# A fused layernorm, banded attention and fp8 linear kernel: another order of loads, other ranks, groups and engine roles

## The chip, the core and the metric

The kernel runs on one core of one Trainium2 chip. The core has five engines with an instruction queue each: TensorE (PE), VectorE (DVE), ScalarE (ACT), GpSimd (POOL) and SyncE (SP), and 16 DMA engines that they share. Each engine takes its instructions in the order in which they were written; between engines semaphores keep the order. The metric is the device time of the kernel in microseconds (us), as the median of several runs. A profiled execution gives the trace from which the tables are read.

## The reference, cut to what matters

```
xn   = layernorm(x)                                   # x: 8 x 512 rows of 1024 float32
attn = einsum('ds,td->st', w1, w2) * sparse_mask      # 1024 x 1024, a band around the diagonal
a    = gelu(einsum('bds,st->bdt', xn, attn) + b2)     # exact gelu
w_q  = fp8_e4m3(weight * 448 / max|weight|)           # one scale for the whole weight
x_q  = fp8_e5m2(xn * 57344 / max|xn|)                 # one scale for all of xn
f    = einsum('bsk,nk->bsn', x_q, w_q) * (1/x_scale) * (1/w_scale) + bias
out  = x + a + f
```

Two maxima are global: the linear part of any row can start only when the largest absolute value of all 4096 normalized rows is known, and the weight can be rounded only when the largest weight is known.

## The kernel before

The 4096 rows are 32 tiles of 128 rows and 1024 columns. Tiles 0 to 15 are *early*: they are loaded once, normalized, transposed, and multiplied by the attn band while the loading goes on. Tiles 16 to 31 are *late*: they are loaded for their statistics and their maximum only, given back, and loaded again when their turn comes.

The work has three stages. In the first, SP loads the x tiles and eight chunks of w1, w2 and the mask; PE makes the band of attn from them, eight chunks of float32 matmuls (`attn_matmuls`, L296), and DVE multiplies each chunk by its mask (`attn_mask`, L307). In the second, the products of the early tiles (`product_matmul`, L518) fill PE, while the maxima of the tiles (`row_max`, L399) and of the weight (`weight_amax`, L448) are taken and the weight is rounded to fp8 values held in bf16. In the third, PE goes through all 32 tiles with the fp8 linear (`linear_matmul`, L558, accumulator `pf`), in 32 steps; the products and transposes of the late tiles are woven into these.

Nothing of this order is written out directly. The kernel lists its operations with an engine, a cost, a rank, what they come after, and which buffers they take and free (`do` of the class `Plan`). `Plan.order` walks through a modelled time and gives each free engine the ready operation of lowest rank; the operations are then emitted in this order, and each engine's queue on the chip is fixed by it. A cost, a lag or a rank changes no computation, only the place in the queues.

The names that the change and the steps below touch:

- `load_order` (L74) gives the order of the loads: for each of the eight attn chunks the chunk, two early x and one late x, with two early x ahead of everything; then the weight once for its maximum ("once"), then again for its rounding ("twice") between late x. Each attn chunk is three loads: w1, the new columns of w2, and the mask.
- `GROUPS` (L35) says which tiles get their inverse root together. The first and last group take it on DVE with one power on POOL (`variance` L336, `power` L340, `inverse_root` L346 to L348, `shifts` L351); the others run eight small instructions on POOL (`inverse_root_gpsimd`, L360 to L369).
- `BY_SCALAR`: early tiles that ACT normalizes (`normalize`, L385); POOL normalizes the others (`normalize_gpsimd`, L394).
- `BY_VECTOR`: early tiles whose second transposed half is moved out of PSUM by DVE (`evict_by_vector`, L505) and not by ACT (`evict_transposed`, L502).
- `B2_BY_TENSOR`: early tiles whose accumulator is started by a matmul with b2 (`b2_matmul`, L513) and not by a copy of ACT (`preload`, L509).
- `ROUNDED_BY_VECTOR`: weight chunks that DVE rounds (L467, L468) and not POOL (`weight_rounded`, L472, L473). Both come after ACT's scaling (L454) and DVE's `weight_magic` (L460, L463).
- `STREAM`: how many late x and "once" weights the planner lets be held at a time.
- `late_amax` (L440), `amax_rows` (L410, which writes `x_mine`), `amax_transpose` (L415, `pt_x`), `amax_row`, `amax_back` and `scale_and_inverse` are the steps to the scale of x. They hop between DVE and PE; `quantize` (L551) and `descale` (L444) follow.

PE's queue holds the transpose `pt_x` in the middle of the early products, and `shifts` of the last group stands on DVE ahead of the steps to the maximum:

```
if lo == 0 or hi == TILES:
    op = do(V, 0.2, 0 if lo == 0 else 99, shifts, lo, hi, after=(op,))
```

Of the kernel before, what the change touches and what calls it, by code (L numbers as in the profile page):

```python
# [23 lines left out]
EARLY = 16  # L24
SLOTS = 34
QUANT = 4
STREAM = 5
LATE = 4

SQUARED = range(EARLY, EARLY + 8)  # L30
BY_VECTOR = range(EARLY // 2, EARLY-5)
B2_BY_TENSOR = range(11, EARLY)
ROUNDED_BY_VECTOR = (6,7)
BY_SCALAR = range(0, 2)
GROUPS = [(0, 2), (2, 4), (4, 8), (8, 12), (12, EARLY), (EARLY, EARLY + 8), (EARLY + 8, 28), (28, 32)]  # L35
TINY = 1e-36
# [35 lines left out]


def load_order():  # L74

    late = iter([*SQUARED, *(i for i in range(EARLY, TILES) if i not in SQUARED)])
    early = iter(range(EARLY))
    found = [("x", next(early)), ("x", next(early))]
    for sc in range(NC):
        found += [("attn", sc)]  # L80
        found += [("x", i) for i in (next(early, None), next(early, None)) if i is not None]
        found += [("x", next(late))]
    found += [("once", c) for c in range(NC)]
    for c in range(NC):
        found += [("twice", c), ("x", next(late))]
    return found
# [90 lines left out]
def banded_path(  # L177
# [264 lines left out]
    def descale():  # L442
        v["descale"] = const.tile([P, 1], F32, name="descale")
        nc.vector.tensor_mul(v["descale"], v["x"][1], v["w"][1])  # L444

# [214 lines left out]
    def more(kind, k):  # L660
        if kind == "x":
            x_ops[k] = load(1.4, load_x, k, take=("slot",) if k < EARLY else ("slot", "stream"))
        elif kind == "attn":
            attn_ops[k] = load(3.0 if k else 3.8, load_attn, k, take=("slot",))
        elif kind == "once":
            w_once[k] = load(1.4, load_weight, k, take=("slot", "stream"))
        else:
            w_twice[k] = load(1.4, load_weight, k, take=("slot", "twice"), after=(w_once[NC - 1],), lag=4.0)

# [19 lines left out]
    for i in range(TILES):  # L689
        if i in SQUARED:  # L690
            m = do(A, 1.6, 5 + 0.01 * i, mean_of, i, after=(x_ops[i],))
            stat[i] = do(A, 1.4, 4, squares, i, after=(m,))
        else:
            stat[i] = do(V, 1.43, 4 + 0.01 * i, statistics, i, after=(x_ops[i],))
    for lo, hi in GROUPS:
        group = [stat[i] for i in range(lo, hi)]
        if 0 < lo and hi < TILES:
            op = do(G, 1.7 + 0.16 * (hi - lo), 0, inverse_root_gpsimd, lo, hi, after=group)
        else:
            op = do(V, 0.2, 0, variance, lo, hi, after=group)  # L700
            op = do(G, 0.4 + 0.16 * (hi - lo), 0, power, lo, hi, after=(op,))
            op = do(V, 0.6, 0, inverse_root, lo, hi, after=(op,))
        for i in range(lo, hi):
            root[i] = shifted[i] = op
        if lo == 0 or hi == TILES:
            op = do(V, 0.2, 0 if lo == 0 else 99, shifts, lo, hi, after=(op,))
            for i in range(lo, hi):
                shifted[i] = op
    maxima, normal, settled = {}, {}, {}
    for i in range(EARLY):  # L710
        if i in BY_SCALAR:
            normal[i] = do(A, 1.14, 3 + 0.01 * i, normalize, i, after=(shifted[i],))
        else:
            normal[i] = do(G, 1.2, 3 + 0.01 * i, normalize_gpsimd, i, after=(shifted[i],))
        maxima[i] = do(V, 1.15, 3 + 0.01 * i, row_max, i, after=(normal[i],))

        settled[i] = do("later", 0.0, i, lambda: None, lag=2.0, after=(normal[i],))
    for i in range(EARLY, TILES):
        ready = stat[i]
        if i not in SQUARED:  # L720
            ready = do(A, 1.14, 3.5, mean_minus, i, after=(ready,))
        maxima[i] = do(V, 1.15, 3 + 0.01 * i, row_max_late, i, after=(ready,), free=("slot", "stream"))
    squared = do(
# [8 lines left out]
    def global_amax(name, fp8_max, rank, cols, after, lag=0.1):  # L732
# [8 lines left out]
    sums = [  # L741
        do(V, 1.15, 2, weight_amax, c, after=(w_once[c],), free=("slot", "stream")) for c in range(NC)
    ]
# [3 lines left out]
    for c in range(NC):  # L747
        op = do(A, 1.1, 1, weight_scaled, c, after=(w_known, w_twice[c]))
# [17 lines left out]
    for i in range(EARLY):  # L766
        in_big = i >= EARLY - NC
        for q in range(2):
# [457 lines left out]
```

## Time and profile before

| what | value |
|---|---|
| median of 3 runs | 317.58 us (317.0 to 317.83) |
| the profiled execution's own time | 316.91 us |
| its span, first to last instruction | 315.0 us |
| mean granted TensorE clock | 0.997 |
| busy: PE, DVE, ACT, POOL | 288.9, 232.0, 158.4, 134.2 us |
| first matmul of attn | 9.98 us |
| first linear matmul (`pf`) | 128.11 us |
| read from and written to HBM | 56.60 and 16.78 MB |

Busy time is the sum of an engine's instructions in the span; PE's matmuls are pipelined, so their lengths overlap a little and a start-to-start distance is the better price of one. A wait is written as the engine and line that stood idle, an arrow, and what ended the idle time, with the total, the number of times and the longest. In the timeline each line gives start and length in us, the engine, the line of the kernel, the operation, and output and input tiles with their shapes. In the rows by window each engine's busy time is followed by the number of its instructions.

### The profile page before, as it was taken

To read this page: it belongs to the slowest core of one execution; us is meant where nothing else is said; L and a number is where in the kernel's file an instruction comes from. 1 tells how busy PE (TensorE), PEld (TensorE's weight loads), DVE (VectorE), ACT (ScalarE), POOL (GpSimd) and SP (SyncE) were. 2 spreads that over 40 slices of the span, in tenths; PEclk is the share of its full clock that TensorE was granted. 3 is DMA by queue.
4 is the path that set the end of the run, shared out by engine and by line. 5 is a ranking of instruction groups with operands and counts; after the bars stand their busy time and mean duration, and the time that the engine had idled before them with its cause. 6 is when DMAs were issued, how large, how long until landed. Compare 5 with 4: busy or idle time off the path is not lost.

```text
span 315.0 us, 4363 instructions
## 1 busy us (share of the span) xinstructions
PE 288.9 (92%) x1563; PEld 216.6 (69%) x1563; DVE 232.0 (74%) x343; ACT 158.4 (50%) x255; POOL 134.2 (43%) x165
## 2 busy tenths in 40 slices
PE   2668889998999979999999999999999999999992
PEld 0657667897998858776676676676667667667651
DVE  3587698999999989756577667767767755766582
ACT  1368369585999956743344424533534442452200
POOL 3151707988488789666311311320331131131160
PEclk9999999999999999999999999999999999999998
DMA  7999999999636747999999987653153332221313
GB/s 251 404 385 379 388 391 390 395 422 417 247 102 230 232 169 108 211 210 271 306 278 305 358 356 236 234 200 135 67 200 135 115 125 99 114 86 67 135 68 141
DMA packets 28509, 73.74 MB, mean 234 GB/s; under 512 B 3392, under 2 KB 11840, under 8 KB 28480
## 3 DMA queue, kind: packets, MB, share of 16 engines
q1 hardware_dynamic: 20992, 47.17, 40.7%
q0 software_dynamic: 2592, 9.44, 15.0%
q10 hardware_dynamic: 4896, 16.78, 13.2%
q8 instruction: 14, 0.23, 0.3%
q14 instruction: 15, 0.12, 0.1%
HBM read 56.60 MB, written 16.78 MB: 233 GB/s over the span
## 4 chain that ended last, share of the span: by engine, by line
PE 59%; DVE 18%; DMA 10%; SPq 5%; ACT 2%; issue 2%; POOL 2%; POOLq 0%
PE pf L558 34%; PE py L518 19%; DMA w<-in_w_dram 8%; DVE row_amax L399 5%; PE pt L493 4%; SPq L262 4%; DVE st L313 3%; DVE w_cols L448 2%; DMA x<-in_x_dram 2%; SPq L253 1%; DVE magic L463 1%; DVE magic L460 1%; PE pa L296 1%; POOL w L472 1%; ACT x L528 1%
## 5 line engine op out<-in xcount | busy, mean ns | idle before, releaser
L558 PE MATMUL pf<-wq,xqts 128*128 128x512 bf16 x504 | 147.8, 379 | 0.0
L518 PE MATMUL py<-attn,xnt 128*128 128x268 f32 (+2 forms) x480 | 117.4, 340 | 2.9 <-ACT py L509 1.6
L518 PEld LDWEIGHTS py<-attn,xnt 128*128 128x128 f32 x480 | 86.7, 190 | 25.7 <-ACT py L509 1.8
L543 POOL TENSOR_TENSOR x<-x,gelu 128x512 f32<-128x512 f32 x32 | 40.8, 1274 | 125.3 <-ACT gelu L540 123.8
L585 DVE SCALAR_TENSOR_TENSOR pf<-pf,descale,bias_bc 128x512 f32<-128x512 f32 x62 | 46.9, 756 | 53.1 <-PE pf L558 53.1
L558 PEld LDWEIGHTS <-xqts 128*128 128x128 fp8e5 x504 | 49.8, 101 | 22.7 <-issue 0.2
L540 ACT ACTIVATE gelu<-py 128x512 f32<-128x512 f32 x32 | 19.1, 598 | 76.5 <-PE py L518 76.5
L588 DVE TENSOR_TENSOR x<-pf,x 128x512 f32<-128x512 f32 x62 | 42.9, 692 | 4.4 <-DVE pf L585 0.5
L399 DVE TENSOR_REDUCE row_amax<-x 128x1 f32<-128x1024 f32 x32 | 37.5, 1200 | 4.5 <-POOL x L394 3.1
L296 PE MATMUL pa<-w_sb,w 128*128 128x268 f32 (+1 forms) x128 | 30.2, 391 | 9.5 <-DMA w_sb<-in_w2t_dram 9.5
L313 DVE BATCH_NORM_STATS2 st<-x 128x6 f32<-128x512 f32 x48 | 30.3, 673 | 9.3 <-DMA x<-in_x_dram 9.3
L502 ACT COPY xnt<-pt 128x512 f32<-128x512 f32 x48 | 27.2, 581 | 16.7 <-PE pt L493 16.7
L296 PEld LDWEIGHTS pa<-w_sb,w 128*128 128x128 f32 x128 | 24.5, 200 | 14.8 <-issue 11.5
L493 PE MATMUL pt<-ident,xn 128*128 128x128 f32 x128 | 33.7, 273 | 0.0
L518 PE MATMUL py<-attn,xnt_big 128*128 128x198 f32 (+2 forms) x160 | 33.2, 343 | 0.0
L509 ACT COPY py<-b_bc 128x512 f32<-128x512 f32 x54 | 32.0, 601 | 1.0
L518 PEld LDWEIGHTS py<-attn,xnt_big 128*128 128x128 f32 x160 | 26.7, 190 | 2.9 <-issue 0.3
L493 PEld LDWEIGHTS pt<-ident,xn 128*128 128x128 f32 x128 | 17.9, 141 | 13.8
L385 ACT ACTIVATE xn<-x,shift,rstd 128x1024 f32<-128x1024 f32 x16 | 19.8, 1240 | 12.9 <-DVE x L588 8.2
L528 ACT ACTIVATE x<-py 128x512 f32<-128x512 f32 x32 | 18.6, 600 | 6.9 <-PE py L518 6.8
L551 DVE TENSOR_SCALAR xqts<-xnt,x_scale 128x1024 fp8e5<-128x1024 f32 x24 | 21.5, 896 | 0.0
L493 PE MATMUL pt<-ident,x 128*128 128x128 f32 x128 | 18.7, 274 | 2.6 <-ACT xnt L502 1.9
(103 smaller groups left out, 239.0 us busy)
## 6 DMA issues: line engine op xcount, KB each, us to landing
x<-in_x_dram SPq DMA_DIRECT2D x48, 512.0 KB, 7.6
out_dram<-x ACTq DMA_DIRECT2D x31, 512.0 KB, 2.6
w<-in_wt_dram SPq DMA_DIRECT2D x16, 512.0 KB, 8.5
x<-in_x_dram POOLq DMA_DIRECT2D x16, 512.0 KB, 19.3
w<-in_w_dram SPq DMA_DIRECT2D x8, 512.0 KB, 9.0
mask<-in_mask_dram SPq DMA_DIRECT2D x8, 512.0 KB, 8.0
w_sb<-in_w2t_dram SPq DMA_DIRECT2D x6, 512.0 KB, 10.7
attn<-in_mask_dram SPq DMA_DIRECT2D x6, 134.0 KB, 9.2
```

The costliest lines, as they stand in the source:

```text
L296: nc.tensor.matmul(pt[:, : hi - lo], w1_sb[:, c, :], w2_sb[:, c, lo:hi], start=(c == 0), stop=(c == NC - 1),)
L313: nc.vector.bn_stats(st[:, h, :], xs[i][:, half(h)])
L399: nc.vector.tensor_reduce(row_amax[:, i : i + 1], xs[i], AX.X, ALU.max, apply_absolute_value=True)
L493: nc.tensor.transpose(pts[i, q][:, j, :], xn[:, c * P : (c + 1) * P], ident)
L502: nc.scalar.copy(xnts[i][:, q * (NC // 2) : (q + 1) * (NC // 2), :], pts.pop((i, q)))
L509: nc.scalar.copy(pys[i, h], b2_bc[:, half(h)])
L518: nc.tensor.matmul(pys[i, h][:, lo - h * HALF : hi - h * HALF], xnts[i][:, sc, :], attn[:, sc, lo - band(sc)[0] : hi - band(sc)[0]], start ...
L528: nc.scalar.activation(xs[i][:, half(h)], pys.pop((i, h)), AF.Gelu)
L543: nc.gpsimd.tensor_add(xs[i][:, half(h)], xs[i][:, half(h)], gelus[i][:, half(h)])
L558: nc.tensor.matmul(v["pf", i, h], v["quant"][:, xqts[i], c, :], wq[:, c, half(h)], start=(c == 0), stop=(c == NC - 1),)
L585: nc.vector.scalar_tensor_tensor(pf, pf, v["descale"], v["bias"][:, half(h)], ALU.mult, ALU.add)
L588: nc.vector.tensor_add(res[:, half(h)], pf, res[:, half(h)])
```

## The change

The loads follow a string of 56 letters: four early x and a late one come ahead of attn's first chunk, and further on early x, late x, attn chunks and weight loads are mixed in another way. The first group of two tiles is split in two groups of one. ACT normalizes seven early tiles in place of two. DVE moves out the second half of nine early tiles in place of three. Four tiles (8, 9, 11, 12) start from a b2 matmul in place of five. DVE rounds weight chunks 5 and 7 in place of 6 and 7. `descale` is written as a multiplication by a scalar column and comes behind the first quantization, and the shift of the last group comes behind the scale of x, with a rank between the quantizations. Ranks, lags and the size of `STREAM` differ.

```diff
-STREAM = 5
+STREAM = 6
-BY_VECTOR = range(EARLY // 2, EARLY-5)
-B2_BY_TENSOR = range(11, EARLY)
-ROUNDED_BY_VECTOR = (6,7)
-BY_SCALAR = range(0, 2)
-GROUPS = [(0, 2), (2, 4), (4, 8), (8, 12), (12, EARLY), (EARLY, EARLY + 8), (EARLY + 8, 28), (28, 32)]
+BY_VECTOR = (2, 6, 7, 8, 10, 11, 12, 14, 15)
+B2_BY_TENSOR = (8, 9, 11, 12)
+ROUNDED_BY_VECTOR = (5, 7)
+BY_SCALAR = (0, 1, 3, 4, 6, 7, 14)
+GROUPS = [(0, 1), (1, 2), (2, 4), (4, 8), (8, 12), (12, EARLY), (EARLY, EARLY + 8), (EARLY + 8, 28), (28, 32)]
...
+ORDER = "eeeelaeaeleeaeaeelalelaeelaleaoleooooooollwllwwlwwwlwllw"
 def load_order():
...
-    found = [("x", next(early)), ("x", next(early))]
-    for sc in range(NC):
-        found += [("attn", sc)]
-        found += [("x", i) for i in (next(early, None), next(early, None)) if i is not None]
-        found += [("x", next(late))]
-    found += [("once", c) for c in range(NC)]
-    for c in range(NC):
-        found += [("twice", c), ("x", next(late))]
+    kinds = dict(
+        a=("attn", iter(range(NC))),
+        e=("x", iter(range(EARLY))),
+        l=("x", late),
+        o=("once", iter(range(NC))),
+        w=("twice", iter(range(NC))),
+    )
+    found = []
+    for ch in ORDER:
+        kind, numbers = kinds[ch]
+        found.append((kind, next(numbers)))
     return found
...
-        nc.vector.tensor_mul(v["descale"], v["x"][1], v["w"][1])
+        nc.vector.tensor_scalar_mul(v["descale"], v["x"][1], v["w"][1])
...
-            w_twice[k] = load(1.4, load_weight, k, take=("slot", "twice"), after=(w_once[NC - 1],), lag=4.0)
+            w_twice[k] = load(1.4, load_weight, k, take=("slot", "twice"), after=(w_once[NC - 1],), lag=5.0)
...
-            m = do(A, 1.6, 5 + 0.01 * i, mean_of, i, after=(x_ops[i],))
-            stat[i] = do(A, 1.4, 4, squares, i, after=(m,))
+            m = do(A, 1.6, 2.5 + 0.01 * i, mean_of, i, after=(x_ops[i],))
+            stat[i] = do(A, 1.4, 3.0, squares, i, after=(m,))
         else:
-            stat[i] = do(V, 1.43, 4 + 0.01 * i, statistics, i, after=(x_ops[i],))
+            stat[i] = do(V, 1.43, (7.0 if i < EARLY else 5.5) + 0.01 * i, statistics, i, after=(x_ops[i],))
...
-        if lo == 0 or hi == TILES:
-            op = do(V, 0.2, 0 if lo == 0 else 99, shifts, lo, hi, after=(op,))
+        if lo == 0:
+            op = do(V, 0.2, 0, shifts, lo, hi, after=(op,))
...
-            normal[i] = do(A, 1.14, 3 + 0.01 * i, normalize, i, after=(shifted[i],))
+            normal[i] = do(A, 1.14, 1.5 + 0.01 * i, normalize, i, after=(shifted[i],))
         else:
-            normal[i] = do(G, 1.2, 3 + 0.01 * i, normalize_gpsimd, i, after=(shifted[i],))
-        maxima[i] = do(V, 1.15, 3 + 0.01 * i, row_max, i, after=(normal[i],))
+            normal[i] = do(G, 1.2, 7.0 + 0.01 * i, normalize_gpsimd, i, after=(shifted[i],))
+        maxima[i] = do(V, 1.15, 4.0 + 0.01 * i, row_max, i, after=(normal[i],))
...
-        maxima[i] = do(V, 1.15, 3 + 0.01 * i, row_max_late, i, after=(ready,), free=("slot", "stream"))
+        maxima[i] = do(V, 1.15, 3.5 + 0.01 * i, row_max_late, i, after=(ready,), free=("slot", "stream"))
...
-        do(V, 1.15, 2, weight_amax, c, after=(w_once[c],), free=("slot", "stream")) for c in range(NC)
+        do(V, 1.15, 3.5, weight_amax, c, after=(w_once[c],), free=("slot", "stream")) for c in range(NC)
...
-        op = do(V, 1.4, 1, weight_magic, c, after=(op,), take=("magic",))
+        op = do(V, 1.4, 4.0, weight_magic, c, after=(op,), take=("magic",))
...
-        op = do(G, 2.55, 1, weight_rounded, c, 0, after=(op, rows_op, root[TILES - 1] if c == 4 else None))
+        op = do(G, 2.55, 1.0, weight_rounded, c, 0, after=(op, rows_op, root[TILES - 1] if c == 5 else None))
...
-            do(G, 2.55, 1, weight_rounded, c, 1, after=(op,), free=("slot", "magic", "twice"), lag=4.0)
-    x_known = global_amax("x", E5M2_MAX, 0, row_amax, (late,), lag=3.0)
-    known = do(V, 0.2, 0.5, descale, after=(x_known,))
+            do(G, 2.55, 1, weight_rounded, c, 1, after=(op,), free=("slot", "magic", "twice"), lag=3.0)
+    x_known = global_amax("x", E5M2_MAX, 0, row_amax, (late,), lag=2.0)
+
+    known = do(V, 0.2, 100.2, descale, after=(x_known,))
+    lo, hi = GROUPS[-1]
+    last_shift = do(V, 0.2, 101.5, shifts, lo, hi, after=(x_known,))
+    for i in range(lo, hi):
+        shifted[i] = last_shift
...
-            evicted[i, q] = do(engine, 0.55, 1.5, emit, i, q, after=(op,), free=("t",))
+            evicted[i, q] = do(engine, 0.55, -5.5, emit, i, q, after=(op,), free=("t",))
...
-                do(A, 0.55, 2 + 0.01 * i, preload, i, h, after=(b2_op,), take=("y",)) for h in range(2)
+                do(A, 0.55, 2.5 + 0.01 * i, preload, i, h, after=(b2_op,), take=("y",)) for h in range(2)
```

More of the change, by code (lines that the diff above doesn't have):

```diff
@@ L71, in band_pieces @@
     ]
+ORDER = "eeeelaeaeleeaeaeelalelaeelaleaoleooooooollwllwwlwwwlwllw"
 def load_order():
     late = iter([*SQUARED, *(i for i in range(EARLY, TILES) if i not in SQUARED)])
-    early = iter(range(EARLY))
-    found = [("x", next(early)), ("x", next(early))]
-    for sc in range(NC):
-        found += [("attn", sc)]
-        found += [("x", i) for i in (next(early, None), next(early, None)) if i is not None]
-        found += [("x", next(late))]
-    found += [("once", c) for c in range(NC)]
-    for c in range(NC):
-        found += [("twice", c), ("x", next(late))]
+    kinds = dict(
[9 more added lines that the diff above has]
+        found.append((kind, next(numbers)))
     return found
@@ L747, in banded_path @@
     for c in range(NC):
-        op = do(A, 1.1, 1, weight_scaled, c, after=(w_known, w_twice[c]))
-        op = do(V, 1.4, 1, weight_magic, c, after=(op,), take=("magic",))
+        op = do(A, 1.1, 1.0, weight_scaled, c, after=(w_known, w_twice[c]))
+        op = do(V, 1.4, 4.0, weight_magic, c, after=(op,), take=("magic",))
         if c in ROUNDED_BY_VECTOR:
```

## The prediction

> **What bounds the kernel now.** I read the page first (busy times, slices), then busy time by stage, then what TensorE waited for, and last the timeline around the longest late wait.
>
> ```profile
> span 315.0 us, 4363 instructions
> PE 288.9 (92%) x1563; PEld 216.6 (69%) x1563; DVE 232.0 (74%) x343; ACT 158.4 (50%) x255; POOL 134.2 (43%) x165
> PE   2668889998999979999999999999999999999992
> DVE  3587698999999989756577667767767755766582
> DMA  7999999999636747999999987653153332221313
> ```
>
> TensorE is nearly full from slice 7 on; what it lacks lies in the first six slices, around slice 15, and at the end. DVE is full from slice 7 to 14. In windows of that shape (busy us of PE, PEld, DVE, ACT, POOL, then clock, DMA share, GB/s):
>
> ```profile
> 0.00:48.00 48.00, 32.76 (x164) 26.44 (x165) 33.28 (x58) 24.07 (x43) 15.34 (x38) 1.00 1.02 367
> 48.00:116.00 68.00, 64.81 (x374) 57.37 (x374) 64.60 (x93) 56.98 (x95) 55.99 (x73) 1.00 0.80 297
> 116.00:130.00 14.00, 12.38 (x70) 10.42 (x71) 12.94 (x20) 9.73 (x14) 13.26 (x14) 1.00 0.71 120
> ```
>
> To 48 us the loads set the pace; to 116 PE and DVE are both full; then PE alone. TensorE's waits up to 128 us:
>
> ```profile
> PE pa L296 <- DMA w_sb<-in_w2t_dram: 9.5, 4, 6.3
> PE pt_x L415 <- DVE x_mine L410: 2.3, 1, 2.3
> PE pt L493 <- ACT xnt L502: 1.9, 1, 1.9
> PE py L518 <- ACT py L509: 1.6, 1, 1.6
> PE py L518 <- ACT xnt L502: 0.7, 1, 0.7
> ```
>
> The second matters most: TensorE stands at the transpose of the x maximum until DVE delivers x_mine. The timeline shows what DVE did before it:
>
> ```profile
> 109.42 0.17 DVE L336 TENSOR_SCALAR var<-mean_var 128x4 f32<-128x4 f32 x1
> 110.74 1.12 DVE L346 TENSOR_TENSOR t<-r 128x4 f32<-128x4 f32 x1 [1.15 <-POOL r L340]
> 112.10 1.01 DVE L348 SCALAR_TENSOR_TENSOR rstd<-t,r 128x4 f32<-128x4 f32 x1
> 113.14 1.08 DVE L351 SCALAR_TENSOR_TENSOR shift<-mean_var,rstd 128x4 f32<-128x4 f32 x1
> 116.57 0.19 DVE L410 TENSOR_REDUCE x_mine<-row_amax 128x1 f32<-128x32 f32 x1
> 116.90 0.27 PE L415 MATMUL pt_x<-ident,x_mine 128*1 128x128 f32 x1 [2.34 <-DVE x_mine L410]
> ```
>
> From the first linear matmul (pf, 128.11 us) two steps take 11.27 us (PE pf L558 x3 at 143.80 and 155.07 in the chain), with no wait. The order of TensorE's instructions from there on is the same in both kernels, so the end moves with that first pf.
>
> **The change part by part.** I set the two instruction orders side by side, engine by engine, and cost them with durations of this trace, start to start where they run back to back.
>
> *Loads.* Five x instead of two go ahead of chunk 0: 3 x 0.524 MB at the 415 GB/s of 9.98 to 14.40 us is 3.8 us, so pa_0 moves from 9.98 to about 13.8. Ahead of chunk 1 stand 6 x instead of 5, of chunk 2 10 instead of 8, and of chunks 3, 4, 5, 6 the same 11, 14, 17, 20; chunk 7 has one fewer. PE's waits for chunks 3, 4, 5 (ends at 33.87, 40.93, 48.01) are DMA's, so those times stay. Up to chunk 3 PE will have done four band pieces fewer (about 1.7 us), because chunk 2 comes some 2 us later. Between chunks 3 and 4 it has 3.7 us of attn, 7 pieces (2.5) and 8 transposes (0.9), 7.1 us for an interval of 7.06; at chunk 5 both orders have done 14 pieces and 52 transposes. So I cost this at nothing. Its cover is the 0.57 and 1.23 us that PE waits at chunks 4 and 5; without it, 1.7 us, which would still meet PE's wait at pt_x. On SP every load still takes its turn, and each issue from the ninth on waits for the eighth before it. POOL's load of b2 (issued at 8.04) moves behind two more groups and tile 2's normalization, to about 14; landing takes 7.2 us, and the first copy of b2 is wanted only beside chunk 2.
>
> The skill speaks against a longer gap here: "TensorE: Matmul & The Clock Gate", What's actually happening, says that after an idle window of about 3.4 us matmuls run at half clock until some 3.4 us of work. The trace agrees: pa_0, after 6.26 idle, takes 4.38 us for 16 matmuls of 198 columns, pa_7 2.84. But that 1.54 us is paid in before already; a gap of 10 us pays it once too. The sum is the same by row and rule here; it matters at pt_x (below).
>
> *Roles.* ACT normalizes 7 early tiles instead of 2 (5 x 1.24 = 6.2 us), POOL 9 instead of 14 (5 x 1.20 less) but one more small group (about 2.7, as 17.42 to 20.12). ACT is half idle to 48 us; only one of the five falls later, with three evictions fewer there. Evictions by DVE go from 3 tiles to 9: five of the six new ones come before x_mine, 5 x 0.60 = **+3.0 us on DVE**. One tile less takes b2 by matmul: PE loses 2 x 0.21, ACT gains 2 x 0.60.
>
> *DVE up to x_mine.* Removed: the last shift, **-1.08**. Between var and t now stand two row maxima and one magic pair, more than POOL's 1.04 for r and its queue: the wait of **1.15** goes. The lengths of t and rstd (1.12, 1.01) are not their own: at 8.10 the same operation took 0.16. They coincide with POOL's additions at 110.69 and 111.92. "SBUF - State Buffer", SBUF: two separate sides, calls the port pair of DVE and GpSimd an exclusive lock, held by one instruction while a DVE operation with two SBUF inputs waits. By the row alone t and rstd keep 2.1 us. By the rule they cost it only while POOL adds; in the new order POOL issues the bias load (0.68) between r and its next addition. The bounds are 0 and **-1.8**; I take -1.8, as DVE should reach t during that issue. Last, DVE's head start: its new order has 38.0 us of work ahead of attn's chunk-5 mask, the old one 35.9. But in it the maximum of tile 8 stands in line behind POOL's normalization (statistics of tile 11 at 45, then 3.2 and 1.2 us: 49.4), while DVE would be there at 46.5. With that 2.9 us and some for ACT's squares I put this mask at 54.0 instead of 52.32; the head start left is **0.6** (0 to 3). Sum for x_mine: 3.0 - 1.08 - 1.15 - 1.8 - 0.6 = **-1.6**, to 115.0.
>
> *From x_mine to pf.* More of the early products stand behind pt_x: 11.4 us against 10.4 by piece (0.45, 0.335 and 0.17 for 268, 198 and 70 columns, 0.44 per four transposes), times the 1.065 that the old stretch really took: **+1.1**. The first late tile's transposes now come inside the products, which removes the 0.70 of PE before 129.19: **-0.7**. Beside it, with cover: DVE has two quantizations more and an eviction ahead of chunk 7's rounding, some 12 us after x_inverse, near 129; chunk 7 is wanted about 4 us after pf starts. POOL's last rounding (chunk 6) ends near 125 instead of 122.3, wanted 3 us after pf. The shift, now behind the second quantization, serves only tiles 28 to 31. descale (1.11) moves behind the first quantization, and total needs it only after eight matmuls. In SP's queue the last late x stands behind weight chunks 4 and 5, which wait for POOL's rounding of the first ones (about 95 us); its statistics come near 106, so 8 us of cover.
>
> Sum: -1.6 + 1.1 - 0.7 = **-1.2 us**. The profiled execution took 316.91 (span 315.0 and 1.91 around it), 0.67 under the median of 317.58, so it would be 315.7; the median **316.4**.
>
> **The rivals.** *The gains cancel.* If POOL's additions meet t and rstd once, or the head start is lost, x_mine moves by about -0.8 and the end by -0.4: 317.2. For it: DVE carries 3.0 us more. Against it: two waits are plainly removed.
>
> *PE becomes the bound.* PE has 1.4 us less ahead of pt_x, so it arrives at 113.2 instead of 114.56. If DVE loses none of its head start (3.0), x_mine is there by then; then the end gains at most 116.9 - 113.2 - 0.4 = 3.3: 314.3. This is the far end of the forecast's case.
>
> *Slower: the wait at pt_x turns the clock down.* If t and rstd stay contended and DVE stands in line as long as I fear, x_mine is not earlier; PE, arriving at 113.2, waits 3.5 us or more. From 3.4 us on the rule above lets the clock fall, and the next products pay pa_0's price: 1.5. End: +0.4 + 1.5 = 319.5, and with x_mine 0.8 late 320.3. In before the wait of 2.34 stayed below: the eight matmuls from 118.83 took their usual 1.74 us. It decides from x_mine at 116.6 on.
>
> *Slower: the late chunk 0 isn't made up.* If ACT's preloads or evictions hold PE between chunks 3 and 5, up to 1.7 us follow to the end: 319.3. The slack at pt_x speaks against it.
>
> **How the numbers follow.** What this kernel's measurement can tell from no change is about 0.3%, 0.95 us. Forecast's case, PE-bound end included: 0.47, own range 314.0 to 316.6. Cancelling: 0.22. Slower by DVE and clock: 0.25; by chunk 0: 0.06. Range 313.6 to 319.8: the low end is the PE-bound case with the 0.7 us at pt_w saved as well, the high end lies between the clock's 319.5 and 320.3.
>
> **What would show it.** pa_0 near 13.8 and chunks 4 and 5 at 41 and 48. DVE without the wait on r; t and rstd at 0.16. x_mine near 115.0, PE's wait there about 1.9 us, pf near 127.6, the same 11.27 per pair after. I am wrong if x_mine is no earlier, if products after pt_x run at half pace, if PE waits between 76 and 112 us on ACT or DVE, or if the stage after pf changes.

## The result, and the profile after

The changed kernel takes 318.36 us (median of 16 executions, 317.54 to 321.59) beside 317.48 us for the kernel before on the same chip: a ratio of 1.0039, 95% interval 1.0021 to 1.0056. It is slower by 0.9 us in the medians, and the whole interval of the ratio lies above 1; the forecast was 316.4, faster. The profiled execution took 319.56 us (before 316.91): the two profiles lie 2.65 us apart, more than the medians, and the part on the clock below says why.

The page of the profile after, its head:

```profile
span 317.8 us, 4364 instructions
PE 291.5 (92%) x1561; PEld 218.0 (69%) x1561; DVE 235.4 (74%) x349; ACT 163.2 (51%) x256; POOL 131.5 (41%) x168
PE   2397999999998879999999999999999999999992
PEclk9999999999999998999999999999999999999999
```

VectorE has 3.4 us more to do, POOL 2.7 less. The clock row has an 8 in its sixteenth slice, just behind pt_x, where before's row has none:

```profile
PEclk9999999999999999999999999999999999999998
```

Of after's waits of TensorE up to 132 us:

```profile
PE pt L499 <- ACT x L391: 7.3, 1, 7.3
PE pt_x L421 <- DVE x_mine L416: 2.1, 1, 2.1
PE py L524 <- ACT py L515: 1.7, 1, 1.7
PE py L519 <- ACT x L534: 1.3, 1, 1.3
```

The first lies in the time of the loads: four transposes now stand there ahead of chunk 0, so that this wait takes over most of the 9.5 us that TensorE waited for chunks before. The wait at pt_x is still there, and the two waits on ScalarE below it are new. The timeline of VectorE ahead of it, and of POOL beside it:

```profile
111.03 0.16 DVE L342 TENSOR_SCALAR var<-mean_var 128x4 f32<-128x4 f32 x1
115.15 0.16 DVE L352 TENSOR_TENSOR t<-r 128x4 f32<-128x4 f32 x1 [0.47 <-POOL r L346]
115.35 1.63 DVE L353 SCALAR_TENSOR_TENSOR t<-t,var 128x4 f32<-128x4 f32 x1
117.01 0.16 DVE L354 SCALAR_TENSOR_TENSOR rstd<-t,r 128x4 f32<-128x4 f32 x1
117.21 1.02 DVE L446 TENSOR_TENSOR row_amax<-row_amax,rstd 128x16 f32<-128x16 f32 x1
118.26 0.19 DVE L416 TENSOR_REDUCE x_mine<-row_amax 128x1 f32<-128x32 f32 x1
...
113.63 1.49 POOL L346 TENSOR_TENSOR r<-var,neg_half 128x4 f32<-128x4 f32 x1
115.78 1.17 POOL L478 TENSOR_TENSOR w<-w,magic 128x512 f32<-128x512 f32 x1
117.03 1.17 POOL L479 TENSOR_TENSOR wq<-w,magic 128x512 bf16<-128x512 f32 x1
```

x_mine comes at 118.26, 1.69 us later than before, not 1.6 earlier. t and rstd are short as forecast, but the second operation of t, and late_amax (0.17 before), now end together with POOL's addition (L478) and subtraction (L479). Then the transpose pt_x in TensorE's timeline, and the clock behind it; rows by window give TensorE's busy time, its instructions, the granted clock, the DMA share and GB/s:

```profile
118.50 0.37 PE L421 MATMUL pt_x<-ident,x_mine 128*1 128x128 f32 x1 [2.14 <-DVE x_mine L416]
```

```profile
118.00:119.00 1.00, 0.50 (x2) 0.74 0.20 78
119.00:120.00 1.00, 1.00 (x5) 0.50 0.42 61
120.00:121.00 1.00, 1.00 (x3) 0.50 0.89 102
121.00:122.00 1.00, 1.00 (x5) 0.55 1.05 209
122.00:123.00 1.00, 1.00 (x8) 1.00 1.13 213
```

Here the clock is at half for some 3.4 us (the four rows lose 1.71 us together). From pt_x to the second pf matmul this execution takes 14.22 us, before 12.73. That matmul starts at 132.72 instead of 129.63: +3.09 = 1.69 (x_mine) - 0.09 (x_mine to pt_x) + 1.49; the two steps behind it take 11.27 us each, as before.

### The profile page after: what moved, and what is told of

It is laid out like the page before. It is cut to its first block, busy times and chain, and to the rows that moved or that the text cites. A ratio compares the mean times of both kernels' runs of the same rounds, so it can differ in the third digit from the quotient of the medians.

```text
span 317.8 us, 4364 instructions
## 1 busy us (share of the span) xinstructions
PE 291.5 (92%) x1561; PEld 218.0 (69%) x1561; DVE 235.4 (74%) x349; ACT 163.2 (51%) x256; POOL 131.5 (41%) x168
## 4 chain that ended last, share of the span: by engine, by line
PE 61%; DVE 11%; POOL 2%; issue 0%
PE pf L564 34%; PE py L524 21%; PE pt L499 5%; DVE row_amax L405 3%; DVE st L319 3%; DVE magic L466 1%; DVE magic L469 1%; DVE xnt_big L511 1%; PE pf L579 1%; DVE mean_var L320 1%; DVE t L353 1%; POOL r L346 0%; POOL x L400 0%; POOL w L478 0%; POOL wq L479 0%; DVE row_amax L446 0%
## 5 line engine op out<-in xcount | busy, mean ns | idle before, releaser
L524 PE MATMUL py<-attn,xnt 128*128 128x198 f32 (+2 forms) x480 | 119.5, 340 | 0.6 <-DVE attn L313 0.4
L524 PE MATMUL py<-attn,xnt_big 128*128 128x198 f32 (+2 forms) x160 | 36.8, 354 | 1.7 <-ACT py L515 1.7
L508 ACT COPY xnt<-pt 128x512 f32<-128x512 f32 x45 | 25.7, 579 | 21.0 <-PE pt L499 21.0
L302 PE MATMUL pa<-w_sb,w 128*128 128x268 f32 (+1 forms) x128 | 31.2, 401 | 3.1 <-DMA w_sb<-in_w2t_dram 3.1
L515 ACT COPY py<-b_bc 128x512 f32<-128x512 f32 x56 | 32.7, 594 | 1.0
L524 PEld LDWEIGHTS py<-attn,xnt_big 128*128 128x128 f32 x160 | 27.9, 198 | 4.3 <-ACT py L515 2.1
L302 PEld LDWEIGHTS pa<-w_sb,w 128*128 128x128 f32 x128 | 25.5, 207 | 7.3 <-issue 4.1
L499 PEld LDWEIGHTS pt<-ident,x 128*128 128x128 f32 x128 | 15.5, 146 | 13.1 <-ACT x L391 8.2
```

Source lines behind the costliest of these rows:

```text
L302: nc.tensor.matmul(pt[:, : hi - lo], w1_sb[:, c, :], w2_sb[:, c, lo:hi], start=(c == 0), stop=(c == NC - 1),)
L499: nc.tensor.transpose(pts[i, q][:, j, :], xn[:, c * P : (c + 1) * P], ident)
L508: nc.scalar.copy(xnts[i][:, q * (NC // 2) : (q + 1) * (NC // 2), :], pts.pop((i, q)))
L515: nc.scalar.copy(pys[i, h], b2_bc[:, half(h)])
L524: nc.tensor.matmul(pys[i, h][:, lo - h * HALF : hi - h * HALF], xnts[i][:, sc, :], attn[:, sc, lo - band(sc)[0] : hi - band(sc)[0]], start ...
```

## The experiments

Seventeen kernels were run. Each is named by the kernel it starts from, `a_` or `e_` from after and `b_` from before. Ratios are to the kernel before on the same chip. "Moves" are made on the planner's finished list, so that only the instructions named change places; what is said of one execution is its profile.

**a_nolock: POOL kept away from the last steps.**

```diff
+        if (c, h) == (4, 1):
...
+            nc.gpsimd.tensor_scalar(junk, row_amax[:, EARLY : EARLY + 1], 1.0, None, ALU.mult)
         nc.gpsimd.tensor_add(w[:, half(h)], w[:, half(h)], magic[:, half(h)])
```

> The kernel after, with one wait more: ahead of the second half of weight chunk 4 GpSimd reads one element of the row maxima into a spare tile, so that its two additions start only when late_amax has run, and VectorE has t, rstd and late_amax without a GpSimd addition beside it. Theory (x_mine came late because these small operations meet GpSimd's additions): the second operation of t falls from 1.63 to about 0.2 us and late_amax from 1.02 to 0.17, x_mine comes about 2.2 us earlier (near 116.0 instead of 118.26), TensorE no longer waits at pt_x (it arrives at 116.4), so the end moves by about 2.0 us, and by up to 3 where the clock fell; about 316.0. GpSimd's last rounding comes some 0.5 us later, which nothing waits for. Rival (the small operations are long for another reason, or the end is set elsewhere): x_mine and the end stay within 0.3 us of after, 318.4.

318.06 us, 1.0016 (0.9997 to 1.0035). Its VectorE, and what TensorE then met:

```profile
116.19 0.16 DVE L352 TENSOR_TENSOR t<-r 128x4 f32<-128x4 f32 x1 [0.47 <-POOL r L346]
116.39 0.16 DVE L353 SCALAR_TENSOR_TENSOR t<-t,var 128x4 f32<-128x4 f32 x1
116.58 0.16 DVE L354 SCALAR_TENSOR_TENSOR rstd<-t,r 128x4 f32<-128x4 f32 x1
116.78 0.17 DVE L446 TENSOR_TENSOR row_amax<-row_amax,rstd 128x16 f32<-128x16 f32 x1
...
133.89 0.38 PE L567 MATMUL pf<-wq,xqts 128*128 128x512 bf16 x1 [0.77 <-DVE wq L474]
```

The operations are at 0.16 and 0.17 once POOL is held back: their length was POOL's. var to x_mine falls from 7.23 to 4.93 us, the 2.3 expected. But the time hardly follows: 0.3 us in the medians, with intervals that overlap. TensorE, held up on ScalarE, is itself only just there (no wait at pt_x any more), and in the profile 0.8 us return as a wait for weight chunk 7. This execution also ran about 1 us later from the loads on.

**a_warm: the wait at pt_x filled.**

```diff
+        for _ in range(8 if name == "x" else 0):
+            nc.tensor.matmul(pt.rearrange("p a b -> p (a b)"), zeros[:, :P], zeros, start=True, stop=True)
         nc.tensor.transpose(pt[:1, 0, :], v[name, "mine"], ident)
```

> The kernel after, with eight matmuls of zeros of 512 columns (about 1.7 us of TensorE) written into the pt_x accumulator just ahead of the transpose pt_x, where TensorE waits 2.1 us anyway. Theory of the clock (part of the loss is the clock that falls after this wait): no slice of the granted clock below 1.0 after pt_x, the products behind it at their usual 0.2 us instead of 0.40, the time about 1 us lower than after in those executions where the clock fell, 0.5 to 1.1 in the median (317.3 to 317.9), and no execution above 319. Rival (the clock falls for another reason, or costs nothing): no change, or up to 0.5 us slower, as the zeros push pt_x back where the wait is shorter.

318.68 us, 1.0029 (1.0014 to 1.0044). In the profile the clock stays at 1.00 and pt_x to the second pf matmul is 12.67 us, 1.55 less than in after's; no execution is above 319.54 where after had four (eight are above 319, against the theory). Yet the median is not lower. Six executions with a mean clock of at least 0.9965 took 318.1 to 319.5: also with a full clock this kernel is slow. The clock alone does not explain after. Why a_warm at full clock is slower still than after at full clock (317.9, in the table below) is not known.

**b_shift: the last shift alone moved, in before.**

```diff
-        if lo == 0 or hi == TILES:
+        if lo == 0:
...
+    last_shift = do(V, 0.2, 101.5, shifts, lo, hi, after=(x_known,))
```

> The kernel before, with one part of the change alone: the last shift moves from ahead of the steps to the maximum to a place behind the first quantizations; the order of every other engine stays as it was. Theory (the end follows x_mine through VectorE's queue): the 1.08 us of the shift leave the path, x_mine comes near 115.5 instead of 116.57, and the end moves with it by about 1.0 us, to 316.5. Rival one (what leaves one small operation goes to the next one, as in after): late_amax or the row maximum meets GpSimd's addition instead and keeps about 1 us; no change. Rival two (the end does not follow x_mine): no change, with x_mine earlier.

317.58 us, 0.9985 (0.9962 to 1.0008): no difference that can be told from noise. x_mine comes at 116.06, only 0.51 us earlier, 0.18 of it from ahead of w_mine. The reason is in two rows:

```profile
113.97 0.68 DVE L460 TENSOR_SCALAR magic<-w 128x1024 int16<-128x1024 int16 x1
114.69 1.26 DVE L463 TENSOR_SCALAR magic<-magic 128x1024 bf16<-128x1024 bf16 x1
...
114.10 1.56 POOL L473 TENSOR_TENSOR wq<-w,magic 128x512 bf16<-128x512 f32 x1
```

The second half of the magic pair took 0.43 us in before; moved up, it meets POOL's subtraction and takes 1.26. What one small operation gives up, the next one pays: rival one, for 0.83 of the 1.08 us.

**b_loads and b_head: the loads.** The first is before with the new string of loads, and the planner's answer to it. The second keeps all of before's order but issues x tiles 2, 3 and 16 ahead of chunk 0.

```diff
+ b_loads:  ORDER and load_order as in after
+ b_head:   load_x 2, 3 and 16 moved ahead of load_attn 0
```

> The kernel before, with the new order of loads alone; roles, groups and ranks stay, though the planner moves some operations in answer. Theory (the loads cost nothing, since chunk 0 near 13.8 us is made up by chunk 5): within 0.5 us of before. Rival (the late chunk 0 is not made up, and after lost its time here): 1 to 2 us slower than before.

> The kernel before with one thing changed: the loads of x tiles 2, 3 and 16 are issued ahead of attn's chunk 0, as in after; every other engine keeps its order. Theory (the late chunk 0 is made up by the DMA-bound chunks 4 and 5): pa_0 near 13.8 us, chunk 4 near 41 and chunk 5 near 48, w_mine near 75.6, pt_x and the end as in before, within 0.3 us. Rival (chunk 0 is not made up): w_mine and pt_x 1 to 2 us later and the time 1 us or more above before.

Both are slower, against the theory: b_loads 320.01 us, 1.0071 (1.0052 to 1.0090), b_head 323.07 us, 1.0165 (1.0129 to 1.0201). A wait of TensorE in b_loads, what ScalarE's timeline shows behind it, and VectorE's longest wait in b_head:

```profile
PE py L518 <- ACT x L533: 4.2, 1, 4.2
```

```profile
110.74 1.15 ACT L459 ACTIVATE w<-w,w_scale 128x1024 f32<-128x1024 f32 x1 [4.14 <-DMA w<-in_wt_dram]
```

```profile
DVE attn L324 <- PE pa L313: 9.9, 2, 8.1
```

In b_loads x_mine is where it was (116.62), but a weight chunk loads later than ScalarE's queue expects it, and the gelu behind it holds TensorE: pt_x only at 121.03, and the clock is at half for 6.8 us from the last part of that wait on. In b_head VectorE stands 8.1 us at chunk 0's mask (the longest of the two waits in the row), with the statistics that it could do meanwhile behind it, and w_mine is at 80.32 instead of 75.62. So the new order of loads costs time unless the ranks fit it. In after's profile they seem to: VectorE is idle for 15.96 us of the first 76, in before for 16.30.

**a_noact, a_both, a_both2: ScalarE's stalls.** Where mean_minus of a late tile waits for VectorE's statistics, a gelu or a preload stands behind it, and TensorE waits for these. The moves:

```diff
+ a_noact:  mean_minus 28 behind gelu_early (6, 0); mean_minus 31 behind preload (10, 0)
+ a_both:   the same, and a_nolock's wait
+ a_both2:  a_both, and mean_minus 30 behind preload (10, 0), mean_minus 31 behind gelu_early (12, 1)
```

> The kernel after with three instructions moved in the emitted order and nothing else: on ScalarE the mean subtraction (mean_minus) of tile 28 goes behind the next gelu and that of tile 31 behind the next preload, where they stood waiting for VectorE's statistics with this gelu and preload stuck behind them; the row maximum of tile 28 follows its subtraction, and VectorE's order stays. Theory (two late arrivals meet at pt_x: VectorE's x_mine at 118.26, TensorE at 116.36, each with its own cause): TensorE's waits of 1.29 and 1.69 us go, it is at pt_x near 113.4, but x_mine stays near 118.2, so the end stays within 0.4 us of after (318.4), or is up to 1 us later where the longer wait of some 5 us turns the clock down. Rival (the waits on ScalarE are what made after slower): the end comes 2 to 3 us earlier, near 316.

> The kernel after with both edits: GpSimd's second half of weight chunk 4 waits for late_amax, and the mean subtractions of tiles 28 and 31 go behind the next gelu and preload. Theory (two late arrivals, neither gives anything alone): x_mine near 116.2 to 117.0, TensorE there at 113.4 to 114.3, the end about 2 us earlier than after and about 1 us earlier than with GpSimd's wait alone: 316.3 to 317.2. A wait of TensorE for wq of chunk 7, which VectorE rounds, of 0.8 us as with GpSimd's wait alone, may take part of it back. Rival (only the waits on ScalarE matter): the same as with the mean subtractions alone. Rival (neither matters): 318.4.

> The kernel after with GpSimd's wait for late_amax, and with ScalarE's order mended further than before, since TensorE still waited 2.2 us for preloads there: now the mean subtractions of tiles 28, 30 and 31 go behind the next gelu or preload, with their row maxima behind them. Theory (two late arrivals at pt_x): TensorE's waits between 100 and 114 us fall from about 2.2 to under 0.7 us, TensorE is at pt_x near 114.5, x_mine as before near 116.8, so pt_x follows x_mine and the end is the same as, or up to 0.4 us earlier than, with the first mending (317.9), since there the two arrived within 0.4 us of each other. Rival (ScalarE's stalls set the end): another 1.5 us earlier.

a_noact: 320.59 us, 1.0098 (1.0071 to 1.0126). a_both: 317.89, 1.0005 (0.9991 to 1.0020). a_both2: 317.73, 1.0013 (1.0003 to 1.0023). In a_noact the stalls only moved, to the next subtraction and preload:

```profile
106.80 1.15 ACT L355 ACTIVATE x<-x,mean_var 128x1024 f32<-128x1024 f32 x1 [1.60 <-DVE mean_var L337]
113.09 2.96 PE L541 MATMUL py<-attn,xnt_big 128*128 128x198 f32 x16 [1.69 <-ACT py L532]
118.70 0.27 PE L438 MATMUL pt_x<-ident,x_mine 128*1 128x128 f32 x1 [2.65 <-DVE x_mine L433]
```

TensorE arrives at 116.05 instead of 116.36 and waits it out at pt_x; x_mine stays (118.46), and the longer wait is paid for in clock: its six executions have mean clocks of 0.988 to 0.992 (319.8 to 320.1 us) or 0.978 to 0.979 (321.1 to 321.5). The stalls cost nothing as long as x_mine is later. With x_mine mended too there is no measurable difference from a_nolock.

**a_evict and e_warm: the evictions.** Tiles 6, 7, 11 and 14 back on ScalarE, at the same place of the list; e_warm adds a_warm's matmuls.

```diff
+        for i in (6, 7, 11, 14):
+            order[at("evict_by_vector", i)].emit = by_scalar
```

> The kernel after with the order of the planner kept, and the second halves of tiles 6, 7, 11 and 14 moved out of PSUM by ScalarE instead of VectorE, at the same place of the emitted order; four of the five evictions that the change put on VectorE ahead of x_mine are so taken back. Theory (VectorE's work ahead of x_mine is what the six new evictions cost): w_mine about 1.2 us earlier (two of them lie ahead of it), x_mine about 2.4 us earlier (near 116.0 where it was 118.3), TensorE is then the bound at pt_x (116.4 and up to 0.6 later for ScalarE's longer queue), and the end 1.5 to 2.5 us earlier than after: 316 to 317. Rival (VectorE waits for loads and for GpSimd up to w_mine anyway): w_mine as in after, x_mine 1.2 us earlier, the end about 1 us earlier, 317.3. Rival (ScalarE's queue holds TensorE up by as much): no change, 318.4.

> The kernel after with the second halves of tiles 6, 7, 11 and 14 moved out by ScalarE, as before (316.5 us at a clock of 0.997 or more, 318.3 at 0.987 to 0.990, 320.1 below), and the eight matmuls of zeros ahead of pt_x, where it waits 2.5 us. Theory (the clock falls behind that wait by chance): one group of times near 316.6, no execution above 318. Rival (the clock falls elsewhere): the three groups stay, median 318.2.

> The kernel before with eight matmuls of zeros of 512 columns written into the pt_x accumulator ahead of the transpose pt_x, where TensorE waits 2.3 us. Of the executions of before some 24% have a mean clock of 0.997 or more and take 316.6 us, some 40% have 0.987 to 0.990 and take 317.7, and 13% less than 0.987 and take 319.1. Theory (the clock falls behind the wait at pt_x, or not, by chance): with the wait filled the slower groups go, the median comes to about 316.6 and the time no longer goes with the clock. Rival (the clock falls elsewhere): the same groups as in before, median 317.5.

a_evict: 318.18 us, 1.0024 (1.0003 to 1.0045). e_warm: 316.99, 0.9980 (0.9966 to 0.9994). b_warm, the same matmuls in before: 316.66, 0.9972 (0.9957 to 0.9988). In a_evict's profile w_mine is at 75.86 and x_mine at 116.81, 1.45 us earlier than in after (2.4 expected). Its median hides that, because its executions lie in groups by their mean clock. Medians in us, with the number of executions:

| kernel (wait at pt_x in its profile) | 0.9965 and more | 0.991 to 0.996 | 0.987 to 0.990 | less |
|---|---|---|---|---|
| before, pooled from three of the series (2.3 us) | 316.62 (38) | 317.47 (37) | 317.69 (65) | 319.07 (21) |
| after (2.1) | 317.93 (3) | 318.26 (10) | 319.56 (2) | 321.59 (1) |
| a_evict (2.5) | 316.54 (7) | 316.57 (2) | 318.34 (8) | 319.84 (4) |
| a_best3, below (none) | 316.61 (5) | 316.38 (10) | 316.59 (7) | |

One execution of a_evict, of 320.86 us, is left out of the table. Where TensorE waits 2 us or more at pt_x, time goes with the clock; where it doesn't, not. With the wait filled the later groups go: 16 of b_warm's 18 executions take 316.4 to 317.0, and all of e_warm's 316.4 to 317.8. b_warm's timeline of TensorE:

```profile
114.11 1.89 PE L416 MATMUL pt_x<-zeros 128*128 128x512 bf16 x7
116.52 0.27 PE L417 MATMUL pt_x<-ident,x_mine 128*1 128x128 f32 x1 [0.51 <-DVE x_mine L410]
```

So the kernel before pays for its wait in most executions, and the one profiled did not. Evictions and clock together, e_warm, take after's whole loss away; in the medians neither does alone.

**a_best, a_best2, a_best3, a_best5, a_best6: a faster version.** From after:

```diff
+ a_best:   a_noact's moves; power r right behind var; t, rstd, late_amax, x_mine right behind the last row maximum;
+           magic 5 behind the scale of x; POOL's subtraction of chunk 4 waits for late_amax; chunk 7 ahead of quantize 2
+ a_best2:  a_both2's order of ScalarE instead of a_noact's
+ a_best3:  a_best2, evictions of tiles 6, 7, 11 on ScalarE
+ a_best5:  a_best3, eviction of tile 15 on ScalarE;  a_best6: it stays on VectorE, ahead of chunk 5's rounding
```

> The kernel after with the mean subtractions of tiles 28 and 31 moved as above, and with VectorE's and GpSimd's last steps before x_mine reordered: the power r right behind var and ahead of weight chunk 4 on GpSimd, t, rstd, late_amax and x_mine straight behind the last row maximum, the magic pair of chunk 5 behind the scale of x, GpSimd's subtraction of chunk 4 waiting for late_amax, and chunk 7 rounded ahead of the third and fourth quantization. Theory (the end follows the later of x_mine and TensorE's arrival at pt_x): x_mine at about 111.1 + 2.3 for two row maxima + 5 small operations of 0.2 = 114.4, TensorE at 113.4, so pt_x about 4 us earlier than in after (114.7 instead of 118.5) and the end 3 to 4 us earlier, 314.5 to 315.5, below before. Rival (what is taken out here returns as a wait for chunks 6 and 7 of the weight when pf starts): a gain of 1 to 2 us only, 316.5 to 317.5, with TensorE waiting for wq.

> The last version with reordered steps before x_mine, now with ScalarE's order mended as in the run above. There x_mine came at 115.28 and TensorE, held up 2.2 us by preloads, only at 116.8. Theory: TensorE near 114.8, so pt_x follows x_mine at about 115.6, 1.2 us earlier, and the end 1.0 to 1.3 us earlier than without the mending: 316.1 to 316.4. Rival (the wait returns behind pt_x, as a wait for weight chunk 6 or 7 when pf starts): the same time as without, 317.4.

> The version of the run above, and the second halves of tiles 6, 7 and 11 moved out by ScalarE instead of VectorE. Theory: x_mine up to 1.8 us earlier still (near 113.5), TensorE near 114.8 then the bound at pt_x, the end 0.5 to 1.0 us earlier than without: 315.3 to 315.9. Rival (ScalarE's longer queue holds TensorE up): the same or 0.5 us slower, with TensorE's waits for ScalarE ahead of pt_x longer by the 1.8 us that it took over.

> The version with reordered steps, mended ScalarE order and tiles 6, 7 and 11 moved out by ScalarE (316.58 us), and now tile 15's second half moved out by ScalarE as well. Theory (the wait of 1.4 us behind pt_x is VectorE's late eviction): it goes, pt_x to the second pf matmul falls from 14.3 to 12.9 us, the end 1.0 to 1.4 us earlier, 315.2 to 315.6. Rival (the rounding of chunk 5 itself holds the next late tile's buffer): the wait stays, under another name, 316.6.

> The same version as the run above starts from, with tile 15's second half still moved out by VectorE, but ahead of the rounding of chunk 5 instead of behind it. Theory (the eviction's place in VectorE's queue): 0.7 to 1.4 us earlier than 316.58, unless chunk 5, rounded 0.7 us later, is late for pf. Rival (the rounding holds the late tile's buffer): the same or up to 0.7 us later than 316.58.

In this order: 317.38 us, 0.9996 (0.9983 to 1.0010); 317.08, 0.9993 (0.9980 to 1.0006); 316.58, 0.9976 (0.9965 to 0.9987); 316.67, 0.9974 (0.9962 to 0.9987); 316.96, 0.9980 (0.9967 to 0.9993). None is as fast as its theory said. a_best3 beats both kernels, and TensorE does not wait at pt_x. Its steps to x_mine, and then what TensorE still waits for in a_best3 and in a_best5:

```profile
113.76 0.15 DVE L384 TENSOR_TENSOR t<-r 128x4 f32<-128x4 f32 x1
114.34 0.17 DVE L478 TENSOR_TENSOR row_amax<-row_amax,rstd 128x16 f32<-128x16 f32 x1
114.55 0.18 DVE L448 TENSOR_REDUCE x_mine<-row_amax 128x1 f32<-128x32 f32 x1
```

```profile
PE pt L534 <- DVE xnt_big L546: 1.4, 1, 1.4
```

```profile
PE pf L599 <- DVE wq L506: 1.2, 1, 1.2
```

x_mine is 3.7 us earlier than in after's profile, the time only 1.8. VectorE's work is late further on instead: in a_best3 tile 15's eviction behind the rounding of chunk 5 (pt_x to the second pf matmul 14.3 us), in a_best5 the rounding of chunk 7 (pt_x to pf 12.7 again, then the wait), in a_best6 a copy on ScalarE (1.6 us). The 1.4 us changed their name.

**b_tail: before with reordered last steps.**

```diff
+ inverse_root behind row_max_late 31; late_amax and x_mine right behind it; shifts behind quantize 1
+ weight_rounded (4, 0) behind x_mine in the list, its subtraction waiting for late_amax
```

> The kernel before with its own loads, roles and ranks, and only the last steps before x_mine reordered: the last row maximum ahead of t, so that it covers the wait of 1.15 us on r; late_amax and x_mine straight behind rstd; the last shift behind the second quantization; GpSimd's subtraction of chunk 4 waiting for late_amax. Theory: x_mine at about 112.0 instead of 116.57 (var 109.4, row maximum 1.2, five small operations of 0.2), TensorE at 114.56 then the bound, so pt_x 2.3 us earlier with no wait in which the clock can fall, and the end 2.3 us earlier than the undisturbed executions of before (316.6): 314.3, up to 315.0 where weight chunks 6 or 7 come late. Rival (a relief of these steps comes back as a later wait, as half of the shift did): 316 to 317.

321.26 us, 1.0113 (1.0087 to 1.0139). From w_mine to x_mine it takes 36.86 us instead of 40.95, as wanted, and then TensorE and ScalarE wait:

```profile
PE py L540 <- ACT xnt L524: 3.8, 1, 3.8
```

```profile
125.04 1.24 ACT L404 ACTIVATE xn<-x,shift,rstd 128x1024 f32<-128x1024 f32 x1 [5.07 <-POOL wq L495]
```

A late tile's normalization waits for POOL's rounding of a weight chunk, and the tile's products stand between the first and the second pf matmul. POOL's wait of 0.7 us for late_amax, and additions that meet VectorE's operations more often, lie ahead of that rounding in its queue; how much of the 3.8 us is theirs was not taken apart.

## Why the prediction was wrong

**Right.** pa_0 came at 14.23 (forecast 13.8), chunks 4 and 5 at 40.81 and 47.87 (41 and 48); the mask of chunk 5 at 53.76 (54.0), tile 8's row maximum at 49.50 (49.4). The order behind pf is unchanged, and the end moved with the second pf matmul: 3.09 us there, 2.8 in the span. descale takes 0.21.

**The step that failed is the sum for x_mine**, above all its term for the port: -1.6 forecast, +1.7 measured, in after's profile against before's:

| term | forecast | measured | how read |
|---|---|---|---|
| evictions on DVE | +3.0 | +2.4 | all of VectorE's busy time ahead of w_mine, three more copies in it, 60.5 instead of 59.3; two more copies of 0.6 behind it |
| head start | -0.6 | -0.3 | idle up to 76 us 15.96 instead of 16.30; my own figures (38.0 - 35.9 and 54.0 - 52.32) give 0.4 and not 0.6 |
| last shift | -1.08 | -1.0 | gone from the queue |
| wait on r | -1.15 | -0.7 | 0.47 left: r, behind chunk 4's first half, ends at 115.1 |
| t, rstd (port) | -1.8 | +0.5 | t to late_amax, start to start plus late_amax, 3.1 instead of 2.6 |
| magic pairs, a row maximum waiting for POOL | 0 | +0.8 | not in the forecast |

The eviction term was the soundest one, and taking most of it back is enough to undo the loss: a_evict takes 1.45 us off x_mine, and its executions at full clock take 316.54 us where after's take 317.93. It is not the only way: a_best2 keeps the evictions, has other steps reordered, and takes 317.08 (0.9993).

The port term was mis-sized by 2.3 us. I let t and rstd escape into POOL's DMA issue and forgot the operations behind them. VectorE did reach t during that issue (115.15, in 115.08 to 115.76), and t and rstd were short. But the second operation of t, recorded from 115.35, 0.43 us ahead of POOL's addition, lasted until that addition's end; so it did, with 1.63 us each, in the four other profiles with this order (a_warm, a_evict, e_warm, a_noact). In a_nolock, where the addition waits, it took 0.16 within the same issue. "SBUF - State Buffer", SBUF: two separate sides, says that whichever of the two engines starts first keeps the port pair for its whole instruction. By the recorded starts VectorE was first here and waited all the same, so how POOL comes to have the port stays open. a_nolock shows that POOL's addition and subtraction made all of the extra length, and b_shift that removing one operation hands most of the conflict to the next while they run back to back. The bound of 0 that I named was not even the bound: the term was a loss.

**TensorE came at 116.36, not 113.2.** Without the two waits on ScalarE (1.29 and 1.69) it would have been 113.4, so the working fits and the waits, which I had named as a sign of being wrong, came. a_noact and a_both2 show that they cost nothing while x_mine is later, and a_best that they count (x_mine 115.28, pt_x 116.81) as soon as it isn't. That the wait at pt_x, 2.14 us, is near the forecast 1.9 (my own terms give 2.1) is luck: both sides came some 3.2 us late.

**From x_mine to pf** I had +0.4; with a full clock it is 12.67 us in a_nolock, a_warm, a_evict and e_warm, 0.06 less than before.

**The clock.** The slower rival had the right chain, x_mine not earlier and half clock behind pt_x, but the wrong point: I let the clock fall only from a wait of 3.4 us on. It fell after 2.14 us here and 2.65 in a_noact, and did not after 2.34 in before's profile and 2.54 in a_evict's. "TensorE: Matmul & The Clock Gate", What's actually happening, also says that the window is free-running; I used its length and not that. Where it asks for a whole idle window, these traces differ: part of one is enough. In each trace every later change of the clock lies a whole multiple of 3.413 us behind the first clock record. These are TensorE's rows around pt_x (busy time, instructions, clock, DMA share, GB/s), cut at such multiples, in after and then in before:

```profile
115.07:118.48 3.41, 1.29 (x8) 1.00 0.47 151
118.48:121.89 3.41, 3.39 (x10) 0.50 0.68 107
```

```profile
111.94:115.35 3.41, 2.62 (x15) 1.00 0.62 252
115.35:118.76 3.41, 1.84 (x10) 1.00 0.00 0
```

After's wait fell whole into one piece, idle for 2.12 us of it, and the next piece ran at half clock; before's longer wait was cut in two at 115.35, and none did. In the nineteen traces together (1655 pieces), of the pieces at full clock none with under 1.8 us idle is followed by half clock, and every one with over 2.0 is; between the two both occur. So a wait of 2 to 2.7 us costs clock or not by where the pieces cut it. That the cut differs from execution to execution fits the table by clock, but each kernel has one trace, so it is not shown.

The price of 1.5 us I had read off pa_0, as paid once whatever the gap. That was wrong. No row shows a low clock there: the rows stand at 1.00, but the first clock record, of full clock, begins only at 12.95 us in before and at 19.49 in after. The lengths fit half clock up to there: pa_0 has 3 of its 4.38 us ahead of that record in before and nearly all of 5.50 in after, about twice the 2.84 of pa_7. So the longer gap cost 1.1 us more; chunks 4 and 5 were in time all the same. That 1.5 fits at pt_x is luck: there the loss is half of one whole piece, 1.71 us, and pt_x to the second pf matmul grew by 1.55 over the 12.67 at full clock.

The clock also spoiled my base: I took the profiled 316.91 for a typical execution 0.67 under the median by scatter, while the median of 317.5 holds the clock's loss and the profile does not. At full clock the change costs 1.3 us (317.93 against 316.62, three executions of after only); the medians show 0.9.

**Left open.** Chunk 5 came between 47.46 and 49.65 us in the profiles with new loads, and between 47.48 and 49.0 in those with the old ones (b_head apart), and w_mine 27.6 to 29.2 us behind it; whether the new order loads a few tenths slower can't be told from one profile each.

## What to carry to other kernels

When an engine's queue sets a wait, count all that the change puts into that queue first, and count a conflict on a shared port as staying until the other engine has no work beside it: shortening one operation hands it on. Where two engines meet at one point, ask when each would be there without the other, since mending one alone gains only up to the second, and look for the next buffer or weight that is late behind it. A wait of TensorE of 2 us can cost up to 1.7 us more in clock, by how it lies to the clock's pieces; compare executions of the same mean clock, and fill such a wait with matmuls of zeros.

## What the runs showed of the hardware

- A fall of TensorE's clock comes in whole pieces of 3.41 us, and follows a piece in which TensorE stood idle for more than about half (1.8 to 2.0 us, worked out above from the nineteen traces). In the profiles of after, a_noact, a_nolock and b_head the windows at a lowered clock lose 1.70 to 1.71 us in all, which is half of 3.41 us; in b_loads, after a wait of 4.15 us, 3.4 us, two pieces. Where it lay at 28 us, in the time of the loads (a_nolock, a_both, a_best2), it cost nothing that could be measured.
- Filling TensorE's wait of 2.3 us with eight matmuls that nobody reads made the kernel before faster by 0.28% (0.12 to 0.43).
- A VectorE operation of 128x4 elements goes from 0.16 us to as much as 1.63 beside POOL's additions, and the second operation of the magic pair, with one input of 128x1024 bf16, from 0.43 to 1.26.
